# A graph network with quantile aggregation on one core: the aggregate put back in node order by one-hot products, pacing marks moved to ScalarE, the layernorm's mean in one pass

## The chip, the core and the metric

The kernel runs on one core of a Trainium2 chip. The metric is the device time of one launch in microseconds (us), taken as the median of several executions. The engines of the core are TensorE (PE, matrix products; its weight loads are listed apart as PEld), VectorE (DVE), ScalarE (ACT), GpSimd (POOL, which here only issues indirect DMAs and small copies) and SyncE (SP, which only issues DMAs). Each engine works through its own instructions in program order, and engines wait for each other through semaphores.

## What is computed

The input holds 16 graphs of 1024 nodes with 64 channels, `x`, and a dense matrix `adj` of 1024 x 1024 for each. Four layers follow one another, each with a layernorm and a relu in front and a residual sum behind:

```
h = max(layernorm(x), 0);  x = x + tanh([h, adj h] W1 + b1) W2 + b2           # layer 0
h = max(layernorm(x), 0);  x = x + (adj h + h) / (row sum of adj + 1)          # layer 1
h = max(layernorm(x), 0);  x = x + mask * (relu((h + agg) W1 + b1) W2 + b2)    # layer 2
h = max(layernorm(x), 0);  x = x + (adj h / column sum of adj) Wn + h Ws + b   # layer 3
```

In layer 2 the graph is first thinned ("dilated": of each node with more than ten neighbours every second or so is dropped, both ways). Then `agg` is, for each node and each channel, a weighted sum (0.25, 0.5, 0.25) of the quartiles over the node's remaining neighbours, with linear interpolation between sorted values. With these inputs a node has some ten to forty neighbours.

## The kernel before

`direct_path` works graph by graph, but six generators (`adjacency`, `layers`, `tail`, `gathers`, `neighbour_lists`, `sorts`) run over the 16 graphs and are interleaved by a small planner at build time (L1447 to L1475). The planner keeps a modelled clock for each engine (`clk.dve`, `clk.pe`, `clk.act`, `clk.pool`). A generator issues some instructions, adds their modelled cost with `after(dve, pe, act, lat)` (L824), and yields the modelled time at which its next DVE instruction may come; `None` means that it waits for another generator, by the set `done`. So the order of the instructions on every engine is fixed at build time by the model, and at run time each engine simply takes them in that order.

- `adjacency(b)` (L941) transposes the matrix on PE, counts neighbours, marks those dropped (`gone`), and builds for each node a row of keys, which goes to DRAM (`keys_d`). It then ranks the nodes by their number of neighbours: `over` counts by eight ACT passes `sink` (L1059), `pos` (L1062) is a node's place in that order, and `low` and `high` are one-hot factors with which PE inverts it into `node` (L1085), the node at each place.
- `neighbour_lists(b)` (L1091) gathers the rows of keys in the order of places (`k`, L1100, by POOL) and takes the largest ones on DVE eight at a time (L1119 to L1134), which gives lists of neighbours, `index`.
- `layers(b)` (L1192) does layers 0 and 1 and the layernorm of layer 2, whose result `h2` is stored to DRAM (`h_d`).
- `gathers(b)` (L1255) fetches the neighbours' rows of `h_d` for five groups of places, 124 indirect DMAs on POOL for each graph (`raw`, L1294). Each group has one buffer, which is free once `sorts` of the graph before is done with it.
- `sorts(b)` (L1311) sorts each group with a network of maxima and minima on DVE (L1327) and sums the wanted places with their weights into `agg` (L1344 to L1350). Nodes with about as many neighbours share a group; that is why `agg` is in the order of places.
- `tail(b)` (L1360) brings the aggregate back into node order and does the rest of layer 2, and layer 3. In the kernel before, `sorts` stores `agg` to `agg_d` (L1355), and `tail` gathers it with eight indirect DMAs on POOL into `res`, by `pos` (L1366). `paired((ha, res), rt)` (L886) then adds `h2` and `res` and transposes them on PE into one bank, and ACT copies that out (L893).

`preln` (L849) is the layernorm: a sum over channels (L854), a small multiplication that makes the mean (L855), the subtraction (L856), a square on ACT (L857), its sum (L859), a root on ACT (L860), a reciprocal (L862), a product (L863) and the relu on ACT (L864). It runs four times for each graph.

`gate()` (L920) paces POOL. When the planner's DVE clock is more than 3 us past the last mark, DVE writes a `mark` of one element (L923) and POOL copies it into `gate` (L925). As POOL takes its instructions in order, what follows on POOL can't start before DVE has come to that point. `gathers` calls it before about every fourth gather, and `neighbour_lists` once for each graph.

The final product of layer 3 (L1403) goes to a PSUM tile `tm`, of which there is one. After the six generators, a flag decides whether a general path (not taken with these inputs) has to run.

Of the kernel before, what the change touches and what calls it, by code (L numbers as in the profile page):

```python
# [7 lines left out]
F32 = mybir.dt.float32  # L8
F16 = mybir.dt.float16
BF = mybir.dt.bfloat16  # L10
I32 = mybir.dt.int32
U16 = mybir.dt.uint16
U8 = mybir.dt.uint8
AF = mybir.ActivationFunctionType
ALU = mybir.AluOpType
AX = mybir.AxisListType

P = 128
C = 64
NB = 8  # L20
N = 1024
# [30 lines left out]
J_ID, J_BIG, J_OFF, J_ST, J_ROW, J_ONE, J_PI, J_NI, J_NEG, J_END = 0, 128, 256, 384, 896, 1920, 2048, 2176, 2184, 2312  # L52
# [680 lines left out]
def direct_path(ctx: ExitStack, tc: tile.TileContext, t: dict, out: bass.AP, flag):  # L733
# [3 lines left out]
    nc = tc.nc  # L737
    x_in, adj, nodemask = t["x"], t["adj"], t["nodemask"]
    B = x_in.shape[0]

    const = ctx.enter_context(tc.tile_pool(name="const", bufs=1))
# [17 lines left out]
    cap8, low8, cn8, half8 = (cf[:, e:e + NB] for e in (E_CAP, E_LOW, E_CN, E_HALF))  # L759
    identh, big_i, offdiag, minus_i = (ch[:, e:e + P] for e in (J_ID, J_BIG, J_OFF, J_NEG))  # L760
    stair, pidx = ch[:, J_ST:J_ST + N // 2], ch[:, J_PI:J_PI + P]
    nid = ch[:, J_NI:J_NI + NB]
    jrow, onerow = ch[0:1, J_ROW:J_ROW + N], ch[0:1, J_ONE:J_ONE + P]
    cols = const.tile([P, 8], F32, name="cols")
    eps, none, wcol = cols[:, :1], cols[:, 1:3], cols[:, 3:6]
# [41 lines left out]

    mask8 = lists.tile([B * NB, P], U8, tag="nbt", name="mask8")
    nc.gpsimd.dma_start(mask8, nodemask.rearrange("b (i p) -> (b i) p", p=P))
    maskf = lists.tile([B * NB, P], F32, tag="ab", name="maskf")  # L810
    nc.vector.tensor_copy(maskf, mask8)
    pm = psum.tile([P, 512], F32, tag="t", name="pt", bufs=3)
    nc.tensor.transpose(pm[:, :B * NB], maskf, identf[:B * NB, :B * NB])
# [7 lines left out]

    clk = Clock()

    def after(dve=0.0, pe=0.0, act=0.0, lat=0.3):  # L824

        clk.dve += dve
        at = clk.dve
        if pe:
            clk.pe = at = max(clk.pe, at) + pe
        if act:  # L830
            clk.act = at = max(clk.act, at) + act
        return at + lat


# [14 lines left out]
    def preln(u, x, ha):  # L849

        s = nodes.tile([P, 4, NB], F32, name="stat")
        xc = mid(u, [P, NB, C])
        sq = mid(u, [P, NB, C])
        nc.vector.tensor_reduce(s[:, 0], x, AX.X, ALU.add)  # L854
        ts(s[:, 1], s[:, 0], 1.0 / C, None, op0=ALU.mult)  # L855
        tt(xc, x, s[:, 1, :, None].to_broadcast([P, NB, C]), ALU.subtract)  # L856
        act(sq, xc, AF.Square)  # L857
        yield after(1.5, act=0.65, lat=1.2)
        nc.vector.tensor_reduce(s[:, 2], sq, AX.X, ALU.add)  # L859
        act(s[:, 3], s[:, 2], AF.Sqrt, bias=eps, scale=1.0 / C)  # L860
        yield after(0.7, act=1.0, lat=1.5)
        nc.vector.reciprocal(s[:, 2], s[:, 3])  # L862
        tt(xc, xc, s[:, 2, :, None].to_broadcast([P, NB, C]), ALU.mult)  # L863
        act(ha[:, :, :C], xc, AF.Relu)  # L864
        yield after(0.9, act=0.65)
# [20 lines left out]
    def paired(hs, dst):  # L886

        p = bank()
        for q in range(4):
            for e, h in enumerate(hs):  # L890
                nc.tensor.matmul(p[:, q * P:(q + 1) * P], h[:, 2 * q:2 * q + 2, :].rearrange("p u c -> p (u c)"), identf,  # L891
                                 start=e == 0, stop=e == len(hs) - 1)
        nc.scalar.copy(dst, p)  # L893
        clk.pe = max(clk.pe, clk.dve) + 2.0 * len(hs)
        clk.act = max(clk.act, clk.pe) + 0.7
# [15 lines left out]
    def even(v, u):  # L911

        return v.rearrange("c (q u p) -> c u q p", u=2, p=P)[:, u]


    marks = []
    slots = const.tile([1, 8], F32, name="mark")
    opened = const.tile([1, 2], F32, name="gate")

    def gate():  # L920
        if not marks or clk.dve > marks[-1] + 3.0:
            k = len(marks)
            nc.vector.memset(slots[:, k % 8:k % 8 + 1], 0.0)  # L923
            clk.dve += 0.15
            nc.gpsimd.tensor_copy(opened[:, k % 2:k % 2 + 1], slots[:, k % 8:k % 8 + 1])  # L925
            marks.append(clk.dve)


    state = [dict() for _ in range(B)]
# [11 lines left out]
    def adjacency(b):  # L941
# [106 lines left out]
        ts(neg, key, -1.0, None, op0=ALU.mult)  # L1048
        p = bank2()
        for q in range(2):  # L1050
            spread = lists.tile([P, 4, P], F32, tag="ab", name="spread")
            tt(spread, identf[:, None, :].to_broadcast([P, 4, P]),
               key[:, 4 * q:4 * q + 4, None].to_broadcast([P, 4, P]), ALU.mult)
            nc.tensor.matmul(p[:, q * 512:(q + 1) * 512], onesf, spread.rearrange("p j m -> p (j m)"),
                             start=True, stop=True)
        over = nodes.tile([P, NB], F32, name="over", bufs=1)
        for i in range(NB):
            sink = lists.tile([P, N], F16, tag="ab", name="sink")
            act(sink, p, AF.Sign, bias=neg[:, i:i + 1], accum_out=over[:, i:i + 1])  # L1059
        yield after(1.6, pe=1.3, act=10.5, lat=2.0)  # L1060
        pos = nodes.tile([P, NB], I32, name="pos", bufs=5)
        ts(pos, over, 0.5, 511.5, op0=ALU.mult, op1=ALU.add)  # L1062

        pi = nodes.tile([P, 2, NB], I32, name="pi", bufs=1)
# [1 line left out]
        ts(pi[:, 1], pos, 7, None, op0=ALU.arith_shift_right)  # L1066
        ph = nodes.tile([P, 2, NB], F16, name="ph", bufs=1)
        nc.vector.tensor_copy(ph, pi)
        low = lists.tile([P, NB, P], F16, tag="ab", name="low")
        tt(low, pidx[:, None, :].to_broadcast([P, NB, P]), ph[:, 0, :, None].to_broadcast([P, NB, P]), ALU.is_equal)  # L1070
        high = nodes.tile([P, NB, NB], F16, name="high", bufs=1)
        tt(high, pidx[:, None, :NB].to_broadcast([P, NB, NB]), ph[:, 1, :, None].to_broadcast([P, NB, NB]),
# [10 lines left out]
        yield after(2.3, pe=1.2, act=0.2) + 1.5  # L1083
        node = nodes.tile([P, NB], I32, name="node", bufs=3)
        nc.vector.tensor_copy(node, p[:, :NB])  # L1085
        clk.dve += 0.1
        g.update(pos=pos, node=node, m=m, keys_d=keys_d)
        done.add(("keys", b))


# [219 lines left out]

    def sorts(b):  # L1311
        g = state[b]
        agg_d = dram.tile([N, C], F32, name="agg_d")
        agg = nodes.tile([P, NB, C], F32, name="agg", bufs=1)
        for k, (b0, n, cap, low, *_) in enumerate(GROUPS):
            while ("gather", b, k) not in done:
                yield None
            raw, at = g.pop(f"raw{k}")
            yield at
            w = n * C  # L1320
            other = work.tile([P, cap, w], F32, tag="other", name="other", bufs=1)
            two = (raw, other)
            program, places = programs[k]
            for greater, s, u, to, (i, j), dims in program:
                vi = [(c, di) for c, di, _ in dims]
                vj = [(c, dj) for c, _, dj in dims]
                tt(view(two[to], *((i, vi) if greater else (j, vj)), w), view(two[s], i, vi, w),  # L1327
                   view(two[u], j, vj, w), ALU.max if greater else ALU.min)
                size = w
                for c, *_ in dims:  # L1330
                    size *= c
                clk.dve += 0.085 + size / 960
                yield clk.dve
            o = sum(len(_wanted(kk, ll)) * m for _, m, kk, ll, *_ in GROUPS[:k])
            wv = g["wts"][:, o:o + len(places) * n].rearrange("p (q i) -> p q i", i=n)

            half = nodes.tile([P, C], F32, name="half", bufs=1)
            sums = [agg[:, b0 + ii] for ii in range(n)] if n == 2 else [agg[:, b0], half]
            for e, (s, i, j) in enumerate(places):
                for ii in range(n):  # L1340
                    v, wq = two[s][:, i, ii * C:(ii + 1) * C], wv[:, j, ii:ii + 1]
                    to = sums[ii if n == 2 else e % 2]
                    if e < 3 - n:
                        ts(to, v, wq, None, op0=ALU.mult)  # L1344
                    else:
                        nc.vector.scalar_tensor_tensor(to, v, wq, to, op0=ALU.mult, op1=ALU.add)  # L1346
                    clk.dve += 0.14
                yield clk.dve
            if n == 1:
                tt(agg[:, b0], agg[:, b0], half, ALU.add)  # L1350
                clk.dve += 0.14
            done.add(("sort", b, k))
            yield clk.dve
        yield clk.dve + 2
        nc.sync.dma_start(agg_d.rearrange("(i p) c -> p i c", p=P), agg)  # L1355
        g.update(agg_d=agg_d, agg_at=clk.dve + 4)
        done.add(("sorts", b))


    def tail(b):  # L1360
        g = state[b]
        x, ha, adjt_d = g["x"], g["h2"], g["adjt_d"]
        yield g["agg_at"]
        res = nodes.tile([P, NB, C], F32, name="res", bufs=1)
        for i in range(NB):
            nc.gpsimd.indirect_dma_start(res[:, i, :], None, g["agg_d"],  # L1366
                                         bass.IndirectOffsetOnAxis(ap=g["pos"][:, i:i + 1], axis=0))
        clk.pool = max(clk.pool, clk.dve) + 10.5
        yield clk.pool + 3.5
        rt = mid(1, [P, 512])  # L1370
        paired((ha, res), rt)
        h1 = big(1, [P, N])
        for u in range(2):
            p = bank()
            nc.tensor.matmul(p, w21[u * C:(u + 1) * C], rt[u * C:(u + 1) * C], start=True, stop=True)
            act(even(h1, u), p.rearrange("p (q m) -> p q m", m=P), AF.Relu, bias=b21)
        y = per_node(bank(), h1, w22, 8, b22)
        yield after(0, pe=6.5, act=2.1) + 6.0
        o = mid(1, [P, NB, C])
        tt(o, y, mask[:, b, :, None].to_broadcast([P, NB, C]), ALU.mult)  # L1380
        tt(x, x, o, ALU.add)
# [47 lines left out]
    found = const.tile([P, FIRST[-1]], F32, name="found")  # L1429
    nc.vector.memset(found, 0.0)  # L1430
    programs = [_program(*group[2:]) for group in GROUPS]
    edge = lists.tile([1, 2, C], F32, tag="ab", name="edge")
    nc.vector.memset(edge[:, 0], 0.0)
    nc.vector.memset(edge[:, 1], BIG)
    h_ds = [dram.tile([N + 2, C], F32, name=f"h_d{k}", bufs=1) for k in range(3)]
# [62 lines left out]
def _constants():  # L1498
# [23 lines left out]
    eh[p, J_OFF + p] = 0  # L1522
    eh[:, J_ST:J_ST + N // 2] = p[:, None] < np.arange(N // 2)
    eh[p, J_ST + p] = 2050
    eh[0, J_ROW:J_ROW + N] = np.arange(N) - 2047
    eh[0, J_ONE:J_ONE + P] = 1
    eh[:, J_PI:J_PI + P] = p
    eh[:, J_NI:J_NI + NB] = p[:, None] + P * np.arange(NB)
# [74 lines left out]
```

## Time and profile before

| | |
|---|---|
| median of 3 executions | 3631.67 us (3631.34 to 3632.71) |
| the profiled execution, its own time | 3640.35 us |
| its span | 3638.5 us |
| busy PE / DVE / ACT / POOL | 1993.7 / 3072.9 / 1410.6 / 2651.7 us |
| share of the span | 55% / 84% / 39% / 73% |
| mean TensorE clock granted | 0.70 of full |
| DVE idle, of which waits that the profile names | 565 us, some 455 us |

The profile is of one execution. The page gives for each engine the busy time, a row of busy tenths over 40 slices of the span, the chain of work that ended last, and groups of instructions (line, engine, operation, output and inputs, shapes, count, then busy us and mean ns, then the engine's idle time just before them and what ended it). A line of the list of waits has the engine and line that waited, what it waited for, and then total us, number of times and the longest. For POOL, the time in which an indirect DMA was being issued is listed as busy, and the time after it, with no visible cause, as "issue". The program starts with one graph's adjacency and layers, in which DVE waits for PE and ACT until 148 us. Then all generators are at work up to about 3300 us, and the last graph's gathers, sorts and tail follow.

### The profile page before, as it was taken

The page shows a single profiled execution, that of the slowest core. Times are in us where ns is not written, and L with a number is a line of the kernel's source. Part 1 is how long each engine was busy: PE and PEld are TensorE (multiplying, and loading weights), DVE is VectorE, ACT ScalarE, POOL GpSimd, SP SyncE. Part 2 cuts the span into 40 slices and gives each one's busy share as a digit, 9 for nine tenths or more (in the row PEclk, how much of TensorE's full clock was granted, in tenths as well). Part 3 has the DMA queues.
Part 4 walks back from the last instruction along what each step waited for, and adds up shares of the span by engine and source line. Part 5 has one row for each costly group of instructions (what it writes and reads, how often), then busy time and mean ns, then how long its engine had stood idle before and what let it go on. Part 6 is the DMA issues. An engine that isn't in the chain of part 4 may idle for free.

```text
span 3638.5 us, 31082 instructions
## 1 busy us (share of the span) xinstructions
PE 1993.7 (55%) x7587; PEld 923.9 (25%) x7587; DVE 3072.9 (84%) x7539; ACT 1410.6 (39%) x2770; POOL 2651.7 (73%) x2777
## 2 busy tenths in 40 slices
PE   6564565746666565746555556765646565550303
PEld 3222222323222222322222222232322322220101
DVE  3497989989898998989798997989898888989662
ACT  5444434344444344353444435443443534330000
POOL 1187787878777787877777787787778777777881
PEclk9676767676676676767676667667667776765555
DMA  2324243342424334151433425243332525232211
GB/s 90 120 62 122 60 129 102 112 129 62 152 66 133 95 109 128 49 184 44 145 81 111 122 72 166 55 134 89 126 109 63 167 56 157 49 123 52 74 27 57
DMA packets 237344, 362.38 MB, mean 100 GB/s; under 512 B 126848, under 2 KB 128496, under 8 KB 237152
## 3 DMA queue, kind: packets, MB, share of 16 engines
q1 hardware_dynamic: 156912, 255.00, 20.2%
q0 software_dynamic: 80096, 104.70, 14.1%
q8 instruction: 62, 1.02, 0.1%
q14 instruction: 130, 1.06, 0.1%
q10 hardware_dynamic: 144, 0.59, 0.0%
HBM read 245.30 MB, written 114.81 MB: 99 GB/s over the span
## 4 chain that ended last, share of the span: by engine, by line
DVE 61%; POOL 11%; issue 11%; DMA 7%; PE 5%; ACT 3%; SPq 0%; DVEq 0%; POOLq 0%; ACTq 0%
DVE raw L1327 16%; DVE other L1327 16%; POOL raw L1294 10%; DVE most L1133 6%; PE pt L883 4%; DVE found L1119 4%; DMA raw<-h_d,index 3%; DVE agg L1346 2%; ACT adjt L1228 2%; DMA k<-keys_d,node 2%; DVE k L1128 2%; DVE nb L948 2%; DVE found L1134 1%; DVE k L1130 1%; DVE gone L1007 1%
## 5 line engine op out<-in xcount | busy, mean ns | idle before, releaser
L1294 POOL DMA_INDIRECT raw<-h_d,index x1984 | 2165.2, 1091 | 558.8 <-issue 498.8
L1327 DVE TENSOR_TENSOR other<-raw 128x512 f32<-128x512 f32 (+11 forms) x816 | 536.4, 688 | 162.5 <-DMA raw<-h_d,index 132.9
L883 PE MATMUL pt<-adjt,ha 128*65 128x512 f32 (+1 forms) x1024 | 492.7, 643 | 91.0 <-DVE ha L1215 68.7
L995 PE MATMUL pt<-eh,nbt 128*128 128x512 f16 (+3 forms) x1024 | 236.6, 379 | 310.2 <-ACT nbt L984 309.7
L1327 DVE TENSOR_TENSOR raw<-other 128x512 f32<-128x512 f32 (+10 forms) x464 | 356.7, 791 | 5.6
L955 PE MATMUL pt<-ef,a 128*128 128x128 f32 x1024 | 205.2, 356 | 220.2 <-ACT adjt L957 136.2
L925 POOL COPY gate<-mark 1x1 f32<-1x1 f32 x462 | 156.4, 339 | 225.0 <-DVE mark L923 217.3
L1133 DVE MAX8 most<-k 128x8 uint16<-128x1024 uint16 x208 | 255.4, 1228 | 7.2
L962 ACT ACTIVATE nb<-nb 128x512 f16<-128x512 f16 x256 | 159.2, 624 | 255.6 <-DVE nb L948 149.6
L883 PEld LDWEIGHTS pt<-adjt,ha 128*65 128x65 f32 (+1 forms) x1024 | 149.9, 150 | 417.6 <-issue 403.3
L955 PEld LDWEIGHTS pt<-ef,a 128*128 128x128 f32 x1024 | 155.6, 183 | 321.6 <-ACT adjt L957 173.9
L995 PEld LDWEIGHTS <-nbt 128*128 128x128 f16 x1024 | 110.4, 120 | 436.0 <-ACT nbt L984 340.7
L1327 DVE TENSOR_TENSOR raw<-other,raw 128x640 f32<-128x640 f32 (+3 forms) x448 | 216.5, 494 | 5.0
L884 ACT COPY big<-pt 64x1024 f32<-64x1024 f32 (+1 forms) x32 | 32.3, 1008 | 476.8 <-PE pt L883 476.8
L1327 DVE TENSOR_TENSOR raw<-raw,other 128x128 f32<-128x128 f32 (+7 forms) x496 | 211.7, 436 | 6.0
L1403 PE MATMUL tm<-at,ha 128*64 128x512 f32 x512 | 175.3, 786 | 74.5 <-DMA at<-adjt_d 74.5
L1002 ACT ACTIVATE gone<-pt,sf 128x512 f16<-128x512 f32 x256 | 161.4, 683 | 124.5 <-DVE sf L976 95.3
L1029 PE MATMUL pt<-eh,gone 128*128 128x128 f16 x1024 | 127.2, 253 | 145.2 <-DVE gone L1007 77.8
L1327 DVE TENSOR_TENSOR other<-other,raw 128x128 f32<-128x128 f32 (+4 forms) x448 | 200.6, 459 | 3.8
L1119 DVE MAX8 found<-k 128x8 f32<-128x1024 f16 x128 | 156.3, 1221 | 51.6 <-DMA k<-keys_d,node 51.6
L891 PE MATMUL pt<-ef,res 128*128 128x128 f32 x128 | 38.9, 399 | 291.9 <-DMA res<-agg_d,pos 291.9
L1034 ACT ACTIVATE nb<-pt 128x1024 f16<-128x1024 f32 x120 | 122.4, 1020 | 164.9 <-PE pt L1032 89.2
(192 smaller groups left out, 4373.6 us busy)
## 6 DMA issues: line engine op xcount, KB each, us to landing
a<-in_adj_dram SPq DMA_DIRECT2D x64, 1024.0 KB
adjt_d<-adjt SPq DMA_DIRECT2D x64, 1024.0 KB
at<-adjt_d SPq DMA_DIRECT2D x128, 512.0 KB
keys_d<-nb SPq DMA_DIRECT2D x64, 512.0 KB
raw<-h_d,index POOLq DMA_INDIRECT x1984
x<-in_x_dram SPq DMA_DIRECT2D x16, 256.0 KB
h_d<-h SPq DMA_DIRECT2D x16, 256.0 KB
agg_d<-agg SPq DMA_DIRECT2D x16, 256.0 KB
```

The lines of the kernel that those rows point to most:

```text
L883: nc.tensor.matmul(p[p0:p0 + n, s], h[:, j, :n], adjt[:, j, s], start=j == 0, stop=j == NB - 1)
L925: nc.gpsimd.tensor_copy(opened[:, k % 2:k % 2 + 1], slots[:, k % 8:k % 8 + 1])
L955: nc.tensor.transpose(p[:, u * P:(u + 1) * P], a[:, j * P:(j + 1) * P], identf)
L962: act(nb[:, i, s], nb[:, i, s], AF.Copy, accum_out=mn[:, q, i:i + 1])
L995: nc.tensor.matmul(p[:, o:e], nbt[:, j, :], stair[:, :e - o], start=j % 4 == 0, stop=j % 4 == 3 and j != i)
L1002: act(gone[:, i, s], p[:, s], AF.Abs, bias=sf[:, 2 + q, i:i + 1], scale=2.0)
L1029: nc.tensor.matmul(p[:, d], gone[:, j, i * P:(i + 1) * P], big_i, start=False, stop=j == 4 * q + 3 and i // 4 != q)
L1119: nc.vector.max(out=eights[0], in_=src)
L1133: nc.vector.max(out=most, in_=less.bitcast(U16))
L1294: nc.gpsimd.indirect_dma_start(raw[:, s, i * C:(i + 1) * C], None, h_ds[b % 3], bass.IndirectOffsetOnAxis(ap=g["index"][:, at:at + 1], axi ...
L1327: tt(view(two[to], *((i, vi) if greater else (j, vj)), w), view(two[s], i, vi, w), view(two[u], j, vj, w), ALU.max if greater else ALU.min)
L1403: nc.tensor.matmul(p[q * C:(q + 1) * C, :], ha[:, j, :], even(ats[j], q), start=j == 0, stop=j == NB - 1)
```

## The change

There are three parts.

The order of the aggregate. `adjacency` keeps, in place of `pos`, a column `place` = 2047 - node for each of the eight blocks of places (the float form of the node's number, read from PSUM; five buffers, while `pos` has one). The constant row `iota` = n - 2047 is filled for all partitions. `sorts` no longer stores `agg`, and `tail` no longer gathers it. Instead, `tail` makes for each block k of 128 places a matrix `hot` of 128 places x 1024 nodes, which is 1 where the node sits at the place, and PE multiplies `agg[:, k]` with it and adds the products in the bank `tm`, after the transposed `h2`. Even blocks of nodes (u = 0) are made by one tensor_scalar on DVE, odd ones (u = 1) by two activations on ACT, Abs(iota + place) and Relu(1 - that). `hot` has two buffers in turn. As `agg` has one buffer, `sorts` of the next graph issues its sums only after the products have been issued (`back`).

The marks. ACT writes them, after each step of the plan with ACT work that ends more than 3 us after the last mark. `gate()` no longer makes a mark; it takes the latest one whose modelled time lies over 1 us before POOL's modelled clock, if it is a new one.

The layernorm. The mean isn't made by itself: one scalar_tensor_tensor computes x - sum / 64.

Besides, the tiles `spread`, `sink`, `low` and three of the start take buffers with the tag `nbt`, where they had a tag `ab` of their own.

```diff
-    nid = ch[:, J_NI:J_NI + NB]
+    nid, iota = ch[:, J_NI:J_NI + NB], ch[:, J_ROW:J_ROW + N]
...
+    marks, gates = [], []
+    slots = const.tile([1, 32], F32, name="mark")
+    opened = const.tile([1, 2], F32, name="gate")
+
+    def mark():
+        if not marks or clk.act > marks[-1][0] + 3.0:
+            t = slots[:, len(marks) % 32:len(marks) % 32 + 1]
+            nc.scalar.copy(t, eps[:1])
+            clk.act += 0.2
+            marks.append((clk.act, t))
+
+    def gate():
+
+        due = [m for m in marks[-20:] if m[0] < clk.pool - 1.0]
+        if due and gates[-1:] != due[-1:]:
+            gates.append(due[-1])
+            nc.gpsimd.tensor_copy(opened[:, len(gates) % 2:len(gates) % 2 + 1], due[-1][1])
...
         if act:
             clk.act = at = max(clk.act, at) + act
+            mark()
...
-        ts(s[:, 1], s[:, 0], 1.0 / C, None, op0=ALU.mult)
-        tt(xc, x, s[:, 1, :, None].to_broadcast([P, NB, C]), ALU.subtract)
+        nc.vector.scalar_tensor_tensor(xc, s[:, 0, :, None].to_broadcast([P, NB, C]), -1.0 / C, x, op0=ALU.mult, op1=ALU.add)
...
-    def gate():
-        if not marks or clk.dve > marks[-1] + 3.0:
-            k = len(marks)
-            nc.vector.memset(slots[:, k % 8:k % 8 + 1], 0.0)
-            clk.dve += 0.15
-            nc.gpsimd.tensor_copy(opened[:, k % 2:k % 2 + 1], slots[:, k % 8:k % 8 + 1])
-            marks.append(clk.dve)
...
-            sink = lists.tile([P, N], F16, tag="ab", name="sink")
+            sink = lists.tile([P, N], F16, tag="nbt", name="sink")
...
-        pos = nodes.tile([P, NB], I32, name="pos", bufs=5)
+        pos = nodes.tile([P, NB], I32, name="pos", bufs=1)
...
+        place = nodes.tile([P, NB], F32, name="place", bufs=5)
+        ts(place, p[:, :NB], -1.0, 2047.0, op0=ALU.mult, op1=ALU.add)
...
+            while b and ("back", b - 1) not in done:
+                yield None
...
-        yield clk.dve + 2
-        nc.sync.dma_start(agg_d.rearrange("(i p) c -> p i c", p=P), agg)
-        g.update(agg_d=agg_d, agg_at=clk.dve + 4)
+        g.update(agg=agg)
...
-        yield g["agg_at"]
-        res = nodes.tile([P, NB, C], F32, name="res", bufs=1)
-        for i in range(NB):
-            nc.gpsimd.indirect_dma_start(res[:, i, :], None, g["agg_d"],
-                                         bass.IndirectOffsetOnAxis(ap=g["pos"][:, i:i + 1], axis=0))
-        clk.pool = max(clk.pool, clk.dve) + 10.5
-        yield clk.pool + 3.5
+        yield clk.dve + 1.0
+
+        agg = g["agg"]
+        p = psum.tile([P, 512], F32, name="tm")
+        for q in range(4):
+            nc.tensor.matmul(p[:, q * P:(q + 1) * P], ha[:, 2 * q:2 * q + 2, :].rearrange("p u c -> p (u c)"), identf,
+                             start=q == 0, stop=False)
+        clk.pe = max(clk.pe, clk.dve) + 2
+        for k in range(NB):
+            for u in range(2):
+                hot = lists.tile([P, 512], F32, name="hot")
+                wide, off = hot.rearrange("p (q m) -> p q m", m=P), g["place"][:, k:k + 1]
+                if u:
+                    act(wide, even(iota, u), AF.Abs, bias=off)
+                    act(hot, hot, AF.Relu, bias=onesf[:, :1], scale=-1.0)
+                else:
+                    ts(wide, even(iota, u), off, 0.0, op0=ALU.add, op1=ALU.is_equal)
+                nc.tensor.matmul(p[u * C:(u + 1) * C, :], agg[:, k, :], hot, start=False, stop=k == NB - 1)
+            clk.act = max(clk.act, clk.dve) + 1.3
+            yield after(0.42, pe=1.5) - 1.5
+        done.add(("back", b))
         rt = mid(1, [P, 512])
-        paired((ha, res), rt)
+        nc.scalar.copy(rt, p)
...
-        yield after(0, pe=6.5, act=2.1) + 6.0
+        yield after(0, pe=6.5, act=3.2) + 6.0
...
-    eh[0, J_ROW:J_ROW + N] = np.arange(N) - 2047
+    eh[:, J_ROW:J_ROW + N] = np.arange(N) - 2047
```

More of the change, by code (lines that the diff above doesn't have):

```diff
@@ L809, in direct_path @@
     nc.gpsimd.dma_start(mask8, nodemask.rearrange("b (i p) -> (b i) p", p=P))
-    maskf = lists.tile([B * NB, P], F32, tag="ab", name="maskf")
+    maskf = lists.tile([B * NB, P], F32, tag="nbt", name="maskf")
     nc.vector.tensor_copy(maskf, mask8)
@@ L913, in even @@
         return v.rearrange("c (q u p) -> c u q p", u=2, p=P)[:, u]
-    marks = []
-    slots = const.tile([1, 8], F32, name="mark")
-    opened = const.tile([1, 2], F32, name="gate")
-    def gate():
-        if not marks or clk.dve > marks[-1] + 3.0:
-            k = len(marks)
-            nc.vector.memset(slots[:, k % 8:k % 8 + 1], 0.0)
-            clk.dve += 0.15
-            nc.gpsimd.tensor_copy(opened[:, k % 2:k % 2 + 1], slots[:, k % 8:k % 8 + 1])
-            marks.append(clk.dve)
     state = [dict() for _ in range(B)]
@@ L1050, in adjacency @@
         for q in range(2):
-            spread = lists.tile([P, 4, P], F32, tag="ab", name="spread")
+            spread = lists.tile([P, 4, P], F32, tag="nbt", name="spread")
             tt(spread, identf[:, None, :].to_broadcast([P, 4, P]),
@@ L1068, in adjacency @@
         nc.vector.tensor_copy(ph, pi)
-        low = lists.tile([P, NB, P], F16, tag="ab", name="low")
+        low = lists.tile([P, NB, P], F16, tag="nbt", name="low")
         tt(low, pidx[:, None, :].to_broadcast([P, NB, P]), ph[:, 0, :, None].to_broadcast([P, NB, P]), ALU.is_equal)
@@ L1085, in adjacency @@
         nc.vector.tensor_copy(node, p[:, :NB])
+        place = nodes.tile([P, NB], F32, name="place", bufs=5)
+        ts(place, p[:, :NB], -1.0, 2047.0, op0=ALU.mult, op1=ALU.add)
         clk.dve += 0.1
-        g.update(pos=pos, node=node, m=m, keys_d=keys_d)
+        g.update(place=place, node=node, m=m, keys_d=keys_d)
         done.add(("keys", b))
@@ L1312, in sorts @@
         g = state[b]
-        agg_d = dram.tile([N, C], F32, name="agg_d")
         agg = nodes.tile([P, NB, C], F32, name="agg", bufs=1)
@@ L1431, in direct_path @@
     programs = [_program(*group[2:]) for group in GROUPS]
-    edge = lists.tile([1, 2, C], F32, tag="ab", name="edge")
+    edge = lists.tile([1, 2, C], F32, tag="nbt", name="edge")
     nc.vector.memset(edge[:, 0], 0.0)
```

## The prediction

> **What bounds the kernel now.** I read the table of engines first, then the costliest groups, then the waits of VectorE (DVE) and GpSimd (POOL), and last the stages in windows of one graph. One graph takes about 213 us: the store of the aggregate (L1355) starts at 636.2, 849.1, 1058.4, 1268.9 and 1481.5 us.
>
> ```profile
> DVE  3497989989898998989798997989898888989662
> POOL 1187787878777787877777787787778777777881
> L1294 POOL DMA_INDIRECT raw<-h_d,index x1984 | 2165.2, 1091 | 558.8 <-issue 498.8
> L925 POOL COPY gate<-mark 1x1 f32<-1x1 f32 x462 | 156.4, 339 | 225.0 <-DVE mark L923 217.3
> ```
>
> The two rows are busy tenths in 40 slices. DVE looks full and POOL looks three quarters full, but POOL's idle time is mostly "issue": about 0.30 us after each indirect DMA, which no wait explains. With it POOL is nearly full too.
>
> ```profile
> 1000.00:1213.00 213.00, 126.67 (x491) 57.47 (x491) 192.65 (x468) 90.74 (x179) 163.14 (x173) 0.72 0.39 113
> ```
>
> The columns are PE, weight loads, DVE, ScalarE (ACT) and POOL busy us. DVE has 193 of 213 us. POOL has 163 us plus some 37 us of issue gaps (the waits list 30 to 35 per 220 us for the raw gathers and 5 for the others), so 200 of 213, or 94%. PE and ACT have slack in the mean. Two full servers hand work to each other: DVE waits for gathered rows, and POOL waits at its gate for DVE.
>
> ```profile
> DVE other L1327 <- DMA raw<-h_d,index: 132.9, 20, 25.7
> DVE found L1119 <- DMA k<-keys_d,node: 51.6, 12, 11.2
> DVE stat L862 <- ACT stat L860: 48.3, 6, 18.1
> DVE stat L859 <- ACT mid L857: 28.8, 6, 9.7
> DVE other L1327 <- issue: 15.5, 5, 6.2
> ...
> POOL gate L925 <- DVE mark L923: 217.3, 51, 129.0
> ```
>
> By windows of 220 us, 68 of the 132.9 us lie after 3300 us, where the adjacency work has ended and POOL alone sets the pace. In the body remain 64 (raw) + 48 (keys, without the first 3.6) + 15.5 (issue) = 128 us of DVE waiting on what POOL delivers. POOL's longest gate wait, 129 us, is the start of the program; 87 us of them are in the body. The last graph ends in a serial chain after its sort:
>
> ```profile
> 3568.94 2.82 DMA agg_d<-agg
> 3571.83 0.70 issue
> 3572.53 0.94 POOL res L1366
> ...
> 3581.27 2.41 DMA res<-agg_d,pos
> 3583.82 0.78 PE pt L891 x2
> 3584.68 0.59 ACT mid L893
> ```
>
> From the last sum of the sort to the copy of the result are 15.7 us (3568.9 to 3584.7).
>
> **The Trainium skill.** (1) "VectorE: DVE Perf Modes", section "The perf-mode tier table": a fp32 tensor_scalar within SBUF runs at twice the rate of a tensor_tensor. The trace agrees: L948, 128x1024, takes 685 ns, L863, a tensor_tensor of 128x512, 693. (2) "ScalarE: Activation LUTs", section "What ACT_TABLE_LOAD costs": 186 ns + 0.833 ns per element, about 93 ns more with a bias column. The trace has 630 ns (L857, 512 elements, no column) and 682 (L1002, with one, from PSUM). (3) The same page, "Table sets": relu and abs are in every set, so the new functions should load no table; the trace has 34 loads, before Sqrt and Tanh but for the first one, and no run yet shows it for Abs beside Relu. (4) "SBUF — State Buffer", section "SBUF: two separate sides": a two-port DVE operation locks GpSimd out, so that descriptors of its DMAs wait. The raw gathers' spread (940 ns least, 1091 mean) fits that.
>
> **The change part by part,** on the profiled execution's own 3640.35 us (span 3638.5).
>
> The reordering leaves POOL. 128 gathers res (L1366) at (135.5 + 34.4)/128 = 1.33 us are 170 us; 120 of them, 159 us, are in the body, 10.6 per graph, and take POOL from 200 to about 189 of 213. SP loses 16 stores agg_d; nobody waits for SP there. The gates stay about as many: I count 35 places per graph, 560 in all, against 462 gates now; up to 100 more at about 0.34 us cost POOL at most 33 us, which the relief covers. What is left on DVE's side then is not POOL's rate but the latency of single groups. I take 70% of the 128 us in the body: -90 us (bounds: -30 and -128). In the stage after 3300 us the eight gathers of the last graph but one stand at 3389 to 3398 us in POOL's unbroken run before a wait of 25.7 us: -10 us.
>
> DVE's own work. Added: 128 tensor_scalar of 128x512 (one of each pair u). No row shows fp16 in and fp32 out. L948's 685 ns at 1024 elements is 533 ns of two elements per cycle and 152 fixed, so 267 + 152 = 419 ns is my estimate, and 0.45 with the gap: +58 us; at one element per cycle, as L1052, 683 ns, +87. Added: 16 small operations place, at 0.2: +3. Removed: 462 marks at 59 ns, -27 by their busy time, though in the sequence they move the next start by only 0.03 to 0.06 us, so I take -20. Removed: 64 of L855, 0.26 us from start to start with the gap: -17. The one-pass subtraction is a scalar_tensor_tensor, which L1239 prices at 691 ns, like L856 now: 0. Sum +24 us, nearly all on the path, since DVE is nine tenths busy.
>
> The new wait. The two tiles hot alternate, so u = 0 is always DVE's buffer and u = 1 ACT's. DVE's step k+1 waits until the product (k, 0) is done, which stands on PE behind (k-1, 1), which waits for ACT's Relu of k-1. Behind the waiting tensor_scalar stands all of DVE's sorting. A round on ACT and PE alone is Abs and Relu at about 0.68 each and a product at 0.64 to 0.69 (L1403: 643 ns median; 175.3 us for 256 pairs of records), with hops about 2.05 us, while the plan paces by 1.5. Over seven rounds that is up to 3.8 us per graph when nothing else delays the plan. But just after the stores of the aggregate PE is working on the keys (L1024 to L1032) in most graphs I looked at (853, 1062, 1269, 1481, 1700, 1909, 2133, 2344 us); the plan then inserts 4.5 us of PE between steps, more than ACT's 2.2 + 1.3, and the stall goes. I take 1 us per graph: +16 (bounds 0 and +112, the latter 7 us per graph, if the eight sinks L1059, 9 us of ACT in one piece, stand in front).
>
> ACT. 256 activations at 0.68 are 174 us, and perhaps 40 marks per graph at 0.17 (L1082: 164 ns) are 110 us: from 91 to about 109 of 213. DVE waits in the body on ACT for about 90 us now; 20% more work in front of it gives +10 (0 to +40). PE gains 256 products at 0.69, 177 us, less the 128 records of res (39 us): about 9 us per graph, beside its 127 of 213. In the start, ACT and PE are in the chain until the lists begin at 148 us; some 35 marks lie there, most of them while ACT waits for PE: +2 (0 to +6).
>
> The end. After the last sum: 0.5 for DVE's step, two products at 0.54 (full clock, as 3621.1), then seven rounds of about 2.05: 16 us, against 15.7: 0, for ACT's step k+1 waits until its one buffer is read. One L855 goes: -0.3.
>
> The moves to the tag nbt (spread, sink, low) join tiles of one stream that run after one another: 0.
>
> Sum: -90 - 10 + 24 + 16 + 10 + 2 = -48, so 3592 for a profiled execution. The median shown, 3631.67, is 8.7 us below the profiled one; on it I forecast 3583 us.
>
> **The rivals.** A, slower: the ping-pong of PE and ACT holds DVE. One mechanism, at the 128 tensor_scalar: at 7 us per graph it costs 112 in place of 16, so -48 + 96 = +48: 3680 us. It decides from 4 us per graph on (16 + 48 = 64 us). For it: the round of 2.05 against 1.5, and waits of DVE on ACT of up to 18.1 us now. Against it: the keys' PE work in that stretch spreads the steps.
> B: ACT's marks hold POOL. ACT waits in order for the messages (L884: 476.8 us over 32, 14.9 each, where the plan has 11.6), and a gate after it waits too; 32 times 3.3 are 106 of the 159 us relieved. A third of the gain is left: -30 - 3 + 24 + 16 + 10 + 2 = +19: 3651 us. For it: POOL now follows an engine that has long waits; against it: a gate asks only for a mark a microsecond or more old, and POOL runs late anyway.
> C: all waits for POOL go, no stall comes: -128 - 25 + 24 + 10 + 2 = -117: 3515 us. Against it: first-row latencies remain.
>
> **How the numbers follow.** Forecast 0.60, A 0.15, B 0.13, C 0.12. The forecast's own range is 3545 to 3625; the one for 8 of 10 is 3525 to 3655, with A's upper part and C's lower left out. A measurement here tells 0.2%, 7 us, from no change. Faster: nearly all of the forecast, C, and a little of A and B in weaker forms: 0.71; same 0.06; slower 0.23.
>
> **What would show it.** POOL in a body graph at 185 to 192 us with its gaps; DVE's waits on raw and k at about 40 us in the body, the new tensor_scalar at 0.42 to 0.45 us; waits of DVE on PE at the new lines below 30 us in all (above 64, A is right); gate waits on ACT marks below 80 us in the body (above 150 with raw waits unchanged, B). The period should come to about 210 us. A clock on PE below 0.65 in the body, or new table loads, would make the sum wrong in a way not listed.

## The result, and the profile after

The changed kernel takes 3951.0 us (median of 4 executions, 3941.9 to 3955.5), where the kernel before took 3632.2 us beside it: a ratio of 1.087, with an interval from 1.086 to 1.089. The forecast was 3583 us, so a gain of 49 us; the change costs 319 us instead. The span of the profiled execution grew from 3638.5 to 3948.0 us.

From the page of the changed kernel, two rows of busy tenths and then groups of instructions (busy us and mean ns, then idle time just before, and its cause):

```profile
DVE  3597979686987968799696987978798696978972
POOL 1276767666576665757566576665757566575670
...
L1387 PE MATMUL tm<-hot,agg 128*64 128x512 f32 x512 | 333.8, 830 | 445.5 <-ACT hot L1384 224.5
...
L841 POOL COPY gate<-mark 1x1 f32<-1x1 f32 x370 | 117.7, 318 | 348.0 <-ACT mark L832 346.7
...
L1386 DVE TENSOR_SCALAR hot<-eh,place 128x512 f32<-128x512 f16 x128 | 65.3, 510 | 236.4 <-PE tm L1387 231.2
```

The row of DVE now dips to 6 again and again, and POOL's is thinner throughout. POOL did what was expected of it: its busy time fell from 2651.7 to 2454.2 us. But it is no longer the partner that DVE waits for most. The longest waits of DVE, in the changed kernel:

```profile
DVE hot L1386 <- PE tm L1387: 231.2, 50, 10.6
DVE agg L1353 <- PE tm L1387: 164.0, 14, 13.3
DVE stat L881 <- ACT stat L879: 71.6, 15, 5.8
DVE other L1334 <- DMA raw<-h_d,index: 52.8, 10, 13.6
DVE found L1127 <- DMA k<-keys_d,node: 50.5, 16, 10.4
```

The wait for gathered rows fell from 132.9 to 52.8 us, as the prediction wanted. How much of this fall is POOL's relief, and how much only DVE's later arrival, is not shown; in e5 below, where DVE is hardly held by the products, the wait is 95.2 us. In its place stand 231 us at the tensor_scalar that makes `hot`, and 164 us at the first sum of the next graph, which overwrites the one `agg` that the last products still read. All waits that the profile names sum to about 721 us in place of 457, and DVE's busy time rose from 3072.9 to 3122.3; 264 + 49 = 313, against 309.5 us of span. So nearly all of the loss is in waits, and the two at the products alone are 395 us.

What a step of the products waits for can be seen on three engines in the same stretch of one graph. PE first (start, length, line, operation; in brackets the idle time before it and its cause):

```profile
1178.45 1.07 PE L1387 MATMUL tm<-hot,agg 128*64 128x512 f32 x2
1182.11 1.07 PE L1387 MATMUL tm<-hot,agg 128*64 128x512 f32 x2 [2.59 <-ACT hot L1384]
1183.11 0.43 PE L1030 MATMUL pt<-nb,eh 128*128 128x512 f16 x1
...
1186.47 0.60 PE L1035 MATMUL pt<-eh,gone 128*128 128x128 f16 x4
1187.01 1.97 PE L1387 MATMUL tm<-hot,agg 128*64 128x512 f32 x2
1190.67 1.97 PE L1387 MATMUL tm<-hot,agg 128*64 128x512 f32 x2 [1.69 <-ACT hot L1384]
```

(Two records make one product here. A product took 1.07 us where the clock granted to PE was 1.00 of full, in the window from 1178 to 1180 us, and 1.97 us where it was 0.50, from 1187 to 1189. In the mean the granted clock was 0.70 before and 0.70 after, so it is not what changed.)

ACT in the same stretch:

```profile
1178.55 1.02 ACT L1040 ACTIVATE nb<-pt 128x1024 f16<-128x1024 f32 x1 [1.54 <-PE pt L1035]
1179.47 1.02 ACT L1045 ACTIVATE pt<-pt 128x1024 f32<-128x1024 f32 x1
...
1180.59 0.72 ACT L1383 ACTIVATE hot<-eh,place 128x512 f32<-128x512 f16 x1
1181.33 0.72 ACT L1384 ACTIVATE hot<-hot,ef 128x512 f32<-128x512 f32 x1
1187.12 1.02 ACT L1040 ACTIVATE nb<-pt 128x1024 f16<-128x1024 f32 x1 [5.06 <-PE pt L1035]
1188.04 1.02 ACT L1045 ACTIVATE pt<-pt 128x1024 f32<-128x1024 f32 x1
```

And DVE:

```profile
1179.56 0.70 DVE L1386 TENSOR_SCALAR hot<-eh,place 128x512 f32<-128x512 f16 x1 [6.06 <-PE tm L1387]
...
1189.02 0.49 DVE L1386 TENSOR_SCALAR hot<-eh,place 128x512 f32<-128x512 f16 x1 [7.44 <-PE tm L1387]
...
1200.65 0.25 DVE L1353 TENSOR_SCALAR agg<-raw,wts 128x64 f32<-128x64 f32 x1 [11.15 <-PE tm L1387]
```

Read it as a circle. PE makes a block of keys (L1030 to L1038). ACT takes it up with two passes of 1.02 us (L1040, L1045), and only then, in its own order, come Abs and Relu (L1383, L1384). The second product of the step waits for the Relu; behind it on PE stands the next block of keys, for which ACT waits in its turn (5.06 us). PE and ACT work by turns: from 1182.1 to 1190.7 a step takes 8.6 us, where the plan counts 4.5 + 1.5 = 6. The plan can't see more: the step's `after(0.42, pe=1.5)` has no time of ACT in it, so no modelled product waits for a Relu. Over a graph the steps fall behind the plan, until DVE, which does follow the plan, meets them, in most graphs at the last two `hot` (6.06 and 7.44 us here) and at `agg` (11.15 us). A graph takes 236 us (first sums at 729.6 and, seven graphs later, at 2381.7 us), where it took about 213.

### The profile page after: what moved, and what is told of

The parts are those of the page before. It is cut to its first block, busy times and chain, and to the rows that moved or that the text cites. A ratio compares the mean times of both kernels' runs of the same rounds, so it can differ in the third digit from the quotient of the medians.

```text
span 3948.0 us, 31775 instructions
## 1 busy us (share of the span) xinstructions
PE 2323.5 (59%) x7971; PEld 957.1 (24%) x7971; DVE 3122.3 (79%) x7157; ACT 1625.5 (41%) x3534; POOL 2454.2 (62%) x2557
## 3 DMA queue, kind: packets, MB, share of 16 engines
q14 instruction: 132, 1.08, 0.1%
## 4 chain that ended last, share of the span: by engine, by line
DVE 39%; PE 25%; ACT 13%; POOL 9%; DMA 6%; issue 6%; SPq 0%; DVEq 0%; POOLq 0%; ACTq 0%
PE pt L902 10%; DVE other L1334 9%; DVE raw L1334 9%; POOL raw L1302 8%; PE tm L1387 5%; DVE most L1141 4%; ACT adjt L1236 3%; DMA k<-keys_d,node 2%; DVE found L1127 2%; DVE agg L1355 2%; ACT hot L1384 2%; DMA raw<-h_d,index 2%; ACT hot L1383 2%; ACT pt L1045 2%; ACT nb L1040 2%
## 5 line engine op out<-in xcount | busy, mean ns | idle before, releaser
L1387 PE MATMUL tm<-hot,agg 128*64 128x512 f32 x512 | 333.8, 830 | 445.5 <-ACT hot L1384 224.5
L1334 DVE TENSOR_TENSOR other<-raw 128x512 f32<-128x512 f32 (+11 forms) x816 | 536.2, 687 | 67.4 <-DMA raw<-h_d,index 52.8
L902 PE MATMUL pt<-adjt,ha 128*65 128x512 f32 (+1 forms) x1024 | 473.7, 623 | 116.7 <-DVE ha L1223 116.7
L1001 PE MATMUL pt<-eh,nbt 128*128 128x512 f16 (+3 forms) x1024 | 255.6, 401 | 311.8 <-ACT nbt L990 311.7
L1108 POOL DMA_INDIRECT k<-keys_d,node x128 | 128.8, 1006 | 370.4 <-DVE found L1142 202.3
L841 POOL COPY gate<-mark 1x1 f32<-1x1 f32 x370 | 117.7, 318 | 348.0 <-ACT mark L832 346.7
L1040 ACT ACTIVATE nb<-pt 128x1024 f16<-128x1024 f32 x120 | 122.7, 1023 | 437.7 <-PE pt L1035 242.7
L1386 DVE TENSOR_SCALAR hot<-eh,place 128x512 f32<-128x512 f16 x128 | 65.3, 510 | 236.4 <-PE tm L1387 231.2
L1424 PE MATMUL tm<-at,ha 128*64 128x512 f32 x512 | 183.5, 812 | 85.0 <-DMA at<-adjt_d 84.9
L961 PEld LDWEIGHTS pt<-ef,a 128*128 128x128 f32 x1024 | 146.5, 176 | 298.5 <-ACT adjt L963 179.1
```

The costliest lines, as they stand in the source:

```text
L902: nc.tensor.matmul(p[p0:p0 + n, s], h[:, j, :n], adjt[:, j, s], start=j == 0, stop=j == NB - 1)
L961: nc.tensor.transpose(p[:, u * P:(u + 1) * P], a[:, j * P:(j + 1) * P], identf)
L1001: nc.tensor.matmul(p[:, o:e], nbt[:, j, :], stair[:, :e - o], start=j % 4 == 0, stop=j % 4 == 3 and j != i)
L1040: act(nb[:, i, :], p, AF.Relu)
L1108: nc.gpsimd.indirect_dma_start(k, None, g["keys_d"], bass.IndirectOffsetOnAxis(ap=g["node"][:, i:i + 1], axis=0))
L1387: nc.tensor.matmul(p[u * C:(u + 1) * C, :], agg[:, k, :], hot, start=False, stop=k == NB - 1)
```

## The experiments

Theory S is the circle just described: the time is set by PE and ACT in series. Theory M says that the shortage of buffers holds DVE. Theory G says that ACT's marks hold POOL at its gate, and POOL holds DVE. Theory R, brought in for e5, says that ACT's added work delays the layernorms in whatever order it comes. Each run was compared with the kernel before on the same chip.

**Buffers.** Three runs give DVE more room and leave the order of ACT alone. e1 has four `hot`, e2 two `agg`, e3 both:

```diff
-                hot = lists.tile([P, 512], F32, name="hot")
+                hot = lists.tile([P, 512], F32, name="hot") if u else mid(1, [P, 512])     # e1, e3
...
-        agg = nodes.tile([P, NB, C], F32, name="agg", bufs=1)
+        agg = nodes.tile([P, NB, C], F32, name="agg", bufs=2)                              # e2, e3
```

> The changed kernel with four tiles hot in place of two: DVE's even ones take turns in two buffers of the tail's scratch, ACT's odd ones keep the two of hot. Theory S (PE and ACT take the products in series, because in ACT's order Abs and Relu of a step stand behind the keys' two passes, and those wait for PE's products of the keys; DVE then runs into the last products by way of hot and of the one agg): DVE's wait at the tensor_scalar hot falls from 236 us to below 80, but the loop ends no earlier, so the wait at the first sum agg grows from 164 to 250 or more; time 3880 to 3950. Theory M (two buffers of hot alone hold DVE): the 236 us go without replacement, 3710 to 3740. Theory G (ACT marks hold POOL and through it DVE): no change beyond 20 us.

> The changed kernel with two buffers for agg, so that the next graph's sums need not wait for the products. Theory S: the wait of 164 us at the first sum goes; the wait at hot stays near 236; 3780 to 3830. Theory M: the wait at agg is only a follower, 3900 or more. Theory G: no change beyond 20 us.

> Both: four tiles hot and two agg. Theory S: DVE no longer meets the products' pace, both waits fall below 60 us together; 3951 - 340 = about 3610 (3570 to 3660), although PE still waits for ACT as long as before (some 220 us). Theory M: 3710 or more. Theory G: 3900 or more.

Measured: e1 3901.4 us (ratio 1.074, 1.072 to 1.077), e2 3912.6 us (1.078, 1.075 to 1.080), e3 3881.9 us (1.070, 1.067 to 1.073). e1 came out as S expected: the wait at `agg` grew to 268.1 us, while that at `hot` fell to 19.4, and the time is not the 3710 to 3740 us of M. e2 and e3 did not come out as S expected: it forecast 3780 to 3830 us for e2 and about 3610 for e3. The waits of DVE in e3:

```profile
DVE stat L878 <- ACT mid L876: 156.4, 14, 13.8
DVE stat L881 <- ACT stat L879: 141.8, 27, 9.3
DVE stat L874 <- ACT x L1218: 71.8, 12, 8.7
DVE other L1334 <- DMA raw<-h_d,index: 54.3, 11, 13.5
```

With all buffers doubled, the waits at the products are gone (21 us are left at `hot`), and DVE waits 370 us in the layernorms instead (77 us at the two of these places that the kernel before shows), for ACT: for their squares (L876) and roots (L879), and for a copy of `x` in front of them (L1218). PE's wait for ACT inside the products is what it was (213.1 us). So the buffers only decided where DVE would wait. M falls; S is left standing, but its part on DVE's side was too narrow, if it is the circle that delays ACT's other work too. R would say that ACT's load does this. e5 and e6 decide between the two.

**ACT out of the circle.** e4 makes the odd matrices by DVE too:

```diff
-                if u:
-                    act(wide, even(iota, u), AF.Abs, bias=off)
-                    act(hot, hot, AF.Relu, bias=onesf[:, :1], scale=-1.0)
-                else:
-                    ts(wide, even(iota, u), off, 0.0, op0=ALU.add, op1=ALU.is_equal)
+                ts(wide, even(iota, u), off, 0.0, op0=ALU.add, op1=ALU.is_equal)
...
-            clk.act = max(clk.act, clk.dve) + 1.3
-            yield after(0.42, pe=1.5) - 1.5
+            yield after(0.95, pe=1.5) - 1.5
```

> The changed kernel with both halves of hot made by DVE's tensor_scalar and none by ACT, two tiles hot and one agg as in the change. Theory S: PE no longer waits for ACT inside the products, so they keep DVE's pace; 128 more tensor_scalar at 0.5 us cost 65 us; the waits at hot and agg fall from 400 to below 150; 3700 to 3780. Theory M: the wait at hot stays or grows, 4000 or more. Theory G: no gain, 3951 + 65.

Measured: 3644.5 us, ratio 1.004 (1.002 to 1.006), 306 us less than the change, with two `hot` and one `agg` as there, though DVE does more; S had expected 3700 to 3780. The two waits in e4:

```profile
DVE hot L1382 <- PE tm L1383: 32.7, 24, 5.3
...
DVE agg L1353 <- PE tm L1383: 16.0, 10, 3.5
```

This takes ACT's work away as well as its place in the order. The next two runs keep the work.

**ACT one step ahead.** e5 and e6 issue Abs and Relu of step k+1 before the products of step k; all the same instructions run. e5 has two `agg`, e6 has one; both have four `hot`:

```diff
+        ahead(0)
         for k in range(NB):
+            ahead(k + 1)
             for u in range(2):
-                hot = lists.tile([P, 512], F32, name="hot")
...
-                if u:
-                    act(wide, even(iota, u), AF.Abs, bias=off)
-                    act(hot, hot, AF.Relu, bias=onesf[:, :1], scale=-1.0)
...
+                hot = odd[k] if u else mid(1, [P, 512])
...
```

Here `ahead(k)` is the pair of activations into a new tile, put into the list `odd`.

> The changed kernel with ACT's Abs and Relu issued one step ahead (those of step k+1 before the product of step k), with four tiles hot and two agg. Theory S (the series of PE and ACT in the products sets the pace): PE finds its odd matrix ready, its wait for ACT inside the products falls from 215 us to below 40, DVE's waits at stat L878 and L881 fall from 300 us (in the run with four hot and two agg) to below 60; as the run with all on DVE less 64 tensor_scalar us: 3560 to 3610. Rival R (ACT's extra load of some 180 us itself delays the layernorm's steps, whatever the order): the waits at stat stay above 200 us, 3750 or more.

> The same with one agg. Theory S: the products no longer trail, so the first sum hardly waits (below 30 us); within 20 us of the run before. Rival R: 3800 or more with 150 us or more at the first sum.

Measured: e5 3578.3 us, ratio 0.986 (0.981 to 0.990), and e6 3587.6 us, 0.987 (0.985 to 0.990). Against e1, which differs from e6 in this order alone, e6 takes 314 us less (3901.4 to 3587.6). Both halves of the circle can be read from the waits, in e1:

```profile
ACT nb L1040 <- PE pt L1035: 227.0, 59, 8.2
...
PE tm L1387 <- ACT hot L1384: 215.3, 98, 4.2
...
ACT nb L1040 <- PE pt L1038: 200.2, 48, 8.2
```

and in e6:

```profile
ACT nb L1040 <- PE pt L1038: 130.8, 53, 8.2
...
ACT nb L1040 <- PE pt L1035: 48.0, 39, 8.2
...
DVE agg L1353 <- PE tm L1395: 46.9, 13, 6.2
...
PE tm L1395 <- ACT hot L1384: 1.7, 4, 0.8
```

PE's wait for ACT in the products fell from 215.3 to 1.7 us (2.3 in e5), and ACT's wait for the keys from 427 to 179 us. This is the run that decides: the same work on every engine, in another order of ACT, and the loss turns into a gain. DVE's waits for the squares and roots are 40 us in e5, against 298 in e3, with all of ACT's work still there. S holds and R falls. e5 is the fastest run that keeps the whole computation. In e6 the single `agg` costs 46.9 us of DVE's waits; the two times differ by 9 us, less than the spread of e5's four (3561 to 3595). How PE runs the products in e5:

```profile
1100.37 0.64 PE L1395 MATMUL tm<-mid,agg 128*64 128x512 f32 x1
1100.38 0.64 PE L1395 MATMUL tm<-hot,agg 128*64 128x512 f32 x1
1100.85 0.59 PE L1395 MATMUL tm<-mid,agg 128*64 128x512 f32 x1
1100.86 0.59 PE L1395 MATMUL tm<-hot,agg 128*64 128x512 f32 x1
```

The halves of a step now start within 0.01 us of each other and take 1.07 us together, at a granted clock of 1.00; in the changed kernel each took 1.07 us alone at that clock. PE's busy time is 2095.0 us in e5 and 2323.5 in the change.

**The marks.** p1 puts the marks of the changed kernel back on DVE, with `gate()` as it was before; p4 puts ACT's marks into the kernel before, by the change's own lines for `mark`, `gate` and `after`.

> The changed kernel with the marks back on DVE, as in the kernel before (a DVE memset each 3 us of the plan and a POOL copy). Theory S: the products rule, 3930 to 3980, with the gate's waits now on DVE. Theory G (ACT's marks hold POOL, and through it DVE): 3700 or less.

> The kernel before with the marks on ACT only. The prediction's terms: -20 on DVE, +10 for ACT's longer queue, +2 in the start: 3615 to 3630. Rival B (ACT marks hold POOL at its gate): gate waits in the body above 150 us, 3660 to 3700.

p1: 3913.1 us, ratio 1.078 (1.075 to 1.080). It is 38 us less than the change, so ACT's marks are not its main fault, and G falls as the cause. POOL's waits at its gate for ACT's marks are long in the changed kernel (346.7 us) and in e1 (316.0), but in e6, with the same marks, they are 9.1 us: they followed from the circle. p4: 3668.5 us, ratio 1.009 (1.007 to 1.010), 33 us slower than the kernel before, where I had -8. The time lies in rival B's range, but its sign is missing: POOL's waits at the gate in the body are 114 us (93 of them for marks) in place of 90 (85 for marks), where B needs 150, and DVE's wait for rows is 119.7 in place of 132.9. Instead, DVE waits longer for ACT at `node` (38.3 against 7.7 us) and `pos` (31.5 against 19.3).

**The layernorm.** p3 is the kernel before with the one-pass mean, by the lines of the diff.

> The kernel before with the one-pass mean only. The prediction's term: 64 small operations of 0.26 us, -17: 3610 to 3620. If it is hidden beside the waits for POOL: 3625 to 3632.

3628.6 us, ratio 0.998 (0.997 to 0.999): 7 us faster, less than the 17 of the sum.

**POOL's relief by itself.** p2 is the kernel before with the eight gathers replaced by one plain load, so the aggregate stays in the order of places. The plan's clocks move with it, so some of the order of issue can change too:

```diff
-        for i in range(NB):
-            nc.gpsimd.indirect_dma_start(res[:, i, :], None, g["agg_d"],
-                                         bass.IndirectOffsetOnAxis(ap=g["pos"][:, i:i + 1], axis=0))
-        clk.pool = max(clk.pool, clk.dve) + 10.5
-        yield clk.pool + 3.5
+        nc.sync.dma_start(res, g["agg_d"].rearrange("(i p) c -> p i c", p=P))
+        yield clk.dve + 4.0
```

> The kernel before with the eight indirect gathers of res replaced by one plain load by SP of the stored aggregate, so that the aggregate stays in the order of places: it leaves the reordering out, and measures what POOL's relief is worth by itself. The prediction's term: DVE's waits on raw and k fall by 90 us and the stage after 3300 us by 10: 3530 to 3550, a little less in the end chain. If POOL isn't the partner that I took it for, but the latency of single gathers: 3600 or more.

3448.6 us, ratio 0.950 (0.948 to 0.951): 182 us, nearly twice what I took for it. Two waits of DVE in p2:

```profile
DVE other L1327 <- DMA raw<-h_d,index: 43.6, 4, 13.6
DVE found L1119 <- DMA k<-keys_d,node: 33.4, 17, 4.3
```

Together with "issue" these were 200 us, and are 81.5. The two waits for ACT in the layernorms, which I had not counted as POOL's, fell from 77 to 4.4 us. DVE's busy time is the same (3072.8 us), so the 192 us of span are all waits. One wait grew, that for the load of `x` at the first sum of a layernorm, from 15.6 to 45.8 us.

**Two variants that remain unexplained.** e7 is e5 with the marks on DVE; e8 is e7 with both halves made by ACT, one step ahead.

> The run with ACT one step ahead and two agg (3578 us), with the marks put back on DVE. If the ACT marks cost something of their own (508 copies in ACT's order, and a POOL that follows ACT's plan in place of DVE's): DVE's waits on raw and keys fall from 167 us to below 110, as in the kernel before without the gather (77), 3520 to 3555. If the marks don't matter: 3560 to 3600.

> The run with ACT ahead, two agg and marks on DVE, with both halves made by ACT (256 more activations of 0.72 us, 128 tensor_scalar of 0.48 us fewer). If DVE's own work is what is left: 61 us less than that run, 3470 to 3510. If ACT in front of the layernorm's steps is: waits at stat rise by 60 us or more, no gain or a loss.

e7: 3656.0 us, ratio 1.006 (1.005 to 1.008), 78 us more than e5 and outside both ranges expected. e8: 3620.8 us, 0.997 (0.996 to 0.998), 35 us less than e7, where either 61 less or no gain was expected. In e7 DVE waits 74.8 us at `pos` for the eight passes `sink`, against 10.6 in e5; in e8 the waits in the layernorms are 163 us against 57 in e7, while DVE's busy time is 50 us less. So marks on DVE are better by 38 us in the changed kernel and worse by 78 in e5, and they were better by 33 in the kernel before. A mark changes the plan's clocks, and with them the order of all instructions; whether its own cost or this reordering is at work, no run here tells apart.

## Why the prediction was wrong

It forecast 3583 us, and 3951 were measured. Step by step:

- **The new wait** is the step that failed. The prediction said that the keys' blocks, 4.5 us of PE between two steps, are "more than ACT's 2.2 + 1.3, and the stall goes". It set ACT's 3.5 us beside PE's, but they stand one after the other, since ACT's two passes wait for the block and the Relu waits behind the passes. What I took for the cover was part of the circle. The price of a product was too low as well: 0.64 to 0.69 us was read from L1403, whose products run in pairs (four records in 1.08 us at 3621.1); alone a product took 1.07 us or more. The term was +16 us; DVE's waits for the products measured 400 us (231.2 and 4.8 at `hot`, 164.0 at `agg`), and e6 against e1 shows 314 us of time from this order alone.
- **Behind the waiting instruction** the prediction named DVE's sorting and looked no further. It left out what stands behind the products on PE and ACT: the next keys, and through ACT the layernorms. e3 shows that part, 370 us of waits, when there are buffers enough at the products.
- **The one `agg`** was not priced. `back` puts the next graph's sums after the products in the order of issue, but the instructions still wait at run time, 164 us in all. Two of them by themselves are worth 38 us (e2), and no clear amount once the circle is broken (e5 against e6).
- **POOL's relief** was right in mechanism and too small in size: -100 against -182 (p2, with what the plan's new order adds). The share of the waits that goes was taken as 70% of those for rows and keys; it was 59% of all of those (200 to 81.5 us), but the waits for ACT went too.
- **DVE's own work:** the tensor_scalar took 0.48 us (median) against an estimate of 0.42. That agrees with the Trainium skill's "VectorE: DVE Perf Modes", section "The perf-mode tier table", in kind, which has a tensor_scalar within SBUF at twice the rate or more: 467 ns at the least is below the 683 that L1052, a tensor_tensor of this size, took. DVE's busy time rose by 49 us, against +24 in the sum. The mean in one pass gave -7 by itself, not -17.
- **ACT:** Abs and Relu took 0.72 us each, where I had 0.68; an estimate from the figures of the Trainium skill's "ScalarE: Activation LUTs", section "What ACT_TABLE_LOAD costs", is 0.186 + 0.833 x 0.512 + 0.093 = 0.706. The table loads stayed at 34, so Abs beside Relu loaded none. There were 508 marks at 0.173 us.
- **The marks** by themselves cost 33 us in p4; the sum had -8 (-20 on DVE, +10 and +2 on ACT).
- **The gates** became 370, not up to 560. Their waits for ACT's marks in the body were 286 us, above the 80 of the forecast and the 150 named for B; but B's other sign, unchanged waits for rows, was missing, and e6, with 9.1 us in all, shows that they followed from the circle.
- **The end:** 16 us were forecast from the last sum to the copy, and about 25 were measured (3873.5 to 3898.8). A round was taken as 2.05 us; it took 2.6, and 3.5 once the products had slowed from 1.07 to 1.97 us.

Rival A named the right place, the products, and the right sign, at 3680 us. Its price, 7 us per graph, came from the eight sinks standing in front; about 25 us of waits per graph were measured (400 over 16 graphs), with the keys in front. Its point of decision, 64 us, was right. Rival B was wrong as a cause, by p1.

That e5, at 3578.3 us, comes out beside the forecast of 3583 is luck. The waits for rows and keys with "issue", which were to fall by 100 us, fell by 31 (200 to 169.3), and DVE's busy time rose by 42 in place of 24; other waits went that the sum had left alone.

Of POOL's 182 us, e5 keeps 52. Between p2 and e5 DVE's busy time differs by 42 us, and its waits for rows and keys by 90 (166.7 against 77.0); the two are about the 130 us that are missing. Why these waits are longer in e5 is open. With the marks on DVE (e7) they are 123.4 us, but then others grow.

## What to carry to other kernels

When an instruction is placed on a second engine to share the load, write down what stands in front of it in that engine's order and what that waits for: two queues that each wait for the other's last piece run in turns, and their times add, however idle both look in the mean (59% and 41% busy here). More buffers only moved the place where the third engine waited; issuing the shared piece one step earlier broke the circle. Measure the gain hoped for by itself, by leaving the work out, before paying for it with a new dependency.

## What was not expected of the hardware

Two products with 64 output rows each, in the upper and the lower half of one bank, ran side by side on PE when both operands were there: 1.07 us for both in e5, and 1.07 us for each when the second came later, all at a granted clock of 1.00. (The kernel before has such pairs at L1403.) So the wait for ACT also lengthened PE's own time at the products: by the windows, PE was busy with them for 333.8 us in the change and 190.1 us in e5. That is 144 of the 228 us of PE's busy time between the two (2323.5 and 2095.0 us). A part of it can be the clock, 0.70 in the mean of the change and 0.73 in that of e5.
